# The second batch's norm, transposes and projections four steps sooner in a hand-written order of layer 0's attention

## The chip, the cores and the metric

The kernel runs on one core of a Trainium2 chip. The metric is the device time of one execution in microseconds (us), the median of several runs. Before the change it is 1410.35 us over three runs (1407.18 to 1412.27).

## The reference, cut to what matters

Four blocks of a small network follow each other on an activation of 4 batches x 256 tokens x 512 features; each adds an attention and a feed-forward result to it. Only the attention of block 0 is touched here:

```python
xn = layernorm(x)                                  # x: (4, 256, 512)
q, k, v = heads(xn @ wq.T), heads(xn @ wk.T), heads(xn @ wv.T)   # 32 heads of 16
q, k = rope(q), rope(k)
scores = where(causal, q @ k.T / sqrt(16), -inf)
out = softmax(scores) @ v
x = x + out @ wo.T + ffn(xn)
```

The four batches are independent of each other up to the sum at the end. The feed-forward part unpacks 4-bit weights; the unpacking is done beside the attention.

## The kernel before, in words

`layer0_attention` (from line 151) runs first, `layer0_ffn` (from line 685) after it, then the other blocks. x is held in eight tiles of 128 tokens, two to a batch. The attention of one batch is cut into four blocks of eight heads, so there are N = 16 blocks, n = 0 to 15, and block n belongs to batch n // 4.

**The order is written out by hand.** Inside `manual_schedule` (line 206) the four compute engines execute their instructions in the order in which the Python code issues them; nothing reorders them. The code walks steps h = -24 to 141 (line 548). `span` is 32 steps, the distance of two batches; two blocks are eight steps apart. In each step the instructions are issued in this order:

1. `selected` (POOL, causal zeroing of one tile of exponentials) for the blocks whose turn it is;
2. the table `first`: scores, transposed maxima, products with the values and what follows them;
3. whatever was booked for this step with `at(h, ...)` in the dictionary `due`: this is where norms, transposes and projections stand;
4. the table `then`: `masked` (DVE, mask and row maximum, two instructions of each of four score tiles);
5. `exponentials` (ACT);
6. in odd steps above 0, one item of `aside`: unpacking of the feed-forward weights, first eight pairs of nibble instructions (line 634) at h = 1 to 15, at h = 17 three DVE instructions (lines 639 to 643) with two stores, from h = 19 on a fetch, a nibble (661), a subtraction (670) and so on.

**A block's steps**, counted from 8n: scores of the second half of the queries at -14 (line 380), maxima at -13 to -11; scores of the first half at -10, maxima at -9 and -8; the maxima transposed on PE at -6 (421, `turn_maxima`), `lowered` on ACT at -5 (426), `joined` on POOL at -3 (431); then the transposed scores `st` at 0 and 4 (439, `turned`), exponentials (449) at 0 to 7, the products with the values `av` at 6 and 10 (469), and their transposes and divisions at 7 and 11 (485, 486, 488, `divided`).

**A batch's own work** is booked ahead of its blocks: `turn(h, b)` (line 244) books the norm of its two tiles on DVE at h (140, `normed`), the four pairs of PE transposes at h + 2 and h + 4 (253), and their copies into `xT` at h + 3 and h + 5, alternating between DVE (98) and ACT (96). `features(h, ...)` (275) books one quarter of the q or the k projection: four matmuls at h (282), the rotation on DVE at h + 1 (293, 293, 295, `rotary`), its sum on POOL at h + 2 (302), and for k two scaled copies on ACT at h + 3 (307). `values(h, ...)` (315) books a half of one tile's v projection: four matmuls (322) and at h + 1 one copy on ACT and one on DVE (333, 334). For batches 1 to 3 the call stands at step 2 of the batch before, with the projections from 7 steps later on. `output` (339) books the product with `wo` of the batch before, at step 17 of a batch.

**PSUM.** Scores use six banks with the tag A. Everything else (projections, transposes, transposed maxima, av) goes through `hb()` (220), which hands out the four halves of two tiles, `half_0` and `half_1`, in the fixed order half_1, half_0, half_1, half_0. Waits are set by tile, not by half: an instruction that reads one half of a tile also waits for a write of the other half that stands ahead of it in the written order.

Of the kernel before, what the change touches and what calls it, by code (L numbers as in the profile page):

```python
# [31 lines left out]
B, T, C = 4, 256, 512  # L32
# [23 lines left out]
def block_stack(ctx: ExitStack, tc: tile.TileContext, d: dict, out: bass.AP):  # L56
# [37 lines left out]
    def evac(i, dst, src):  # L94
        if i % 2:
            nc.scalar.copy(dst, src)
        else:
            nc.vector.tensor_copy(dst, src)
# [33 lines left out]
    def normed(t, moments, patterns):  # L132

        xn = lnp.tile([P, C], F32, tag="xn", name=f"xn_{t}")
        dst, src = xn, x_sb[:, t, :]
        if patterns:
            before, after, sizes = patterns
            dst = xn.rearrange(after, **sizes)
            src = src.rearrange(before, **sizes)
        nc.vector.tensor_scalar(dst, src, *moments[t], ALU.subtract, ALU.mult)  # L140
        return xn
# [9 lines left out]
    def layer0_attention(hook, aside, xp, wd):  # L151
# [13 lines left out]
        with (  # L165
# [54 lines left out]
            def hb():  # L220

                turns.append(0)
                return halves[len(turns) * 2 % 4 + len(turns) // 2 % 2]
# [3 lines left out]
            def at(h, *fs):  # L227
                due.setdefault(h, []).extend(fs)
# [15 lines left out]
            def turn(h, b):  # L244

                for k, t in enumerate((2 * b, 2 * b + 1)):
                    had = {}

                    def half(c0, t=t, had=had):
                        tp = had[c0] = hb().rearrange("p (c i) -> p c i", c=2)  # L250
                        for c in range(2):
                            f = slice((c0 + c) * P, (c0 + c + 1) * P)
                            nc.tensor.transpose(tp[:, c, :], had["xn"][:, f], ident)

                    def copy(c0, t=t, had=had):
                        evac(c0 // 2, xT[:, c0 : c0 + 2, t * P : (t + 1) * P], had[c0])

                    at(h, lambda t=t, had=had: had.update(xn=normed(t, mom, patterns)))
                    for c0 in (0, 2):
                        at(h + 2 + 2 * k, lambda c0=c0, f=half: f(c0))  # L260
                        at(h + 3 + 2 * k, lambda c0=c0, f=copy: f(c0))
# [234 lines left out]
            span = 8 * NC  # L496

            def halves_of_x():
                x = [
                    xp.tile([P, NC, 512], F32R, tag=f"x{i}", name=f"x_{n}_{i % 2}")  # L500
                    for i, n in enumerate(("hi", "hi", "lo", "lo"))
                ]
                return x[:2], x[2:]

            def split(half, c):
                x = xT[:, c, half * 512 : half * 512 + 512]
                eng = (nc.vector, nc.gpsimd)[half]
                nc.scalar.copy(hi[half][:, c], x)
                eng.tensor_tensor(lo[half][:, c], x, hi[half][:, c].bitcast(F32), ALU.subtract)

            end = 8 * N + 6
            batches = [Batch(0)]
# [34 lines left out]
            with start_order:  # L547
                for h in range(-24, end + 8):
                    b, k = divmod(h, span)
                    if k == 2 and 0 <= b < B - 1:  # L550


                        turn(h, b + 1)
                        batches.append(Batch(b + 1))
                        u, h0 = batches[-1], h + 7
                        for i in range(4):
                            u.features(h0 + 2 * i, i % 2, i // 2)
                        for i in range(2):
                            u.features(h0 + 16 + 2 * i, i, 2)
                            u.values(h0 + 20 + 2 * i, i, 0)  # L560
                            u.features(h0 + 24 + 2 * i, i, 3)
                            u.values(h0 + 28 + 2 * i, i, 1)
                    if k == (17 if b < 3 else 14) and 1 <= b < B:

                        for i in range(4):
                            batches[b - 1].output(h + (2 if b < 3 else 4) * i, i // 2, i % 2)
                    if h == 8 * N - 22:
                        hi, lo = halves_of_x()
                        for i in range(8):
                            at(h + 2 * i, lambda i=i: split(i % 2, i // 2))  # L570
                    if (h + 14) % 8 == 0 and 0 <= (h + 14) // 8 < N:
                        blocks.append(Block((h + 14) // 8))
                    now = [(h - 8 * n, x) for n, x in enumerate(blocks)]
                    for o, x in now:
                        if 0 <= o - 1 < 8:
                            x.selected(*divmod(o - 1, 4))
                    for o, x in now:
                        if o in first:
                            first[o](x)
                    for f in due.pop(h, ()):  # L580
                        f()
                    for o, x in now:
                        if o in then:
                            then[o](x)
                    for o, x in now:
                        if 0 <= o < 8:
                            x.exponentials(o % 4)
                    if h % 2 == 1 and h > 0 and aside:
                        aside.pop(0)()
                assert not aside and not due  # L590
                return hi, lo, [batches[-1].output(None, i // 2, i % 2) for i in range(4)]
# [1540 lines left out]
    with (  # L2132
        tc.tile_pool(name="gu", bufs=1) as gup,
        tc.tile_pool(name="gur", bufs=2) as raw,
        tc.tile_pool(name="gus", bufs=READY) as ready,
        tc.tile_pool(name="guh", bufs=1) as held,
        tc.tile_pool(name="dram", bufs=1, space=bass.MemoryType.DRAM) as dram,
    ):
        gu = GateUp(gup, raw, ready, held, dram)
        aside = []  # L2140

        def hook():
            gu.load()
            aside.extend(gu.points())
            for blk in range(NBLK):
                aside.extend(gu.pieces(blk))

        def layer1_begun():
            pools = [
                early.enter_context(tc.tile_pool(name=n, bufs=k, side="right"))  # L2150
                for n, k in (("w1", 1), ("l1", 1))
            ]
            begun.append(Layer1(layer1_weights(pools[0]), pools[1]))
            return begun[0]

        with tc.tile_pool(name="wd", bufs=1) as wdp, ExitStack() as x2:
            wd = wdp.tile([P, NBLK, C], F32, name="wd")
            xp = x2.enter_context(tc.tile_pool(name="x2", bufs=1, side="right"))
            begin = layer0_attention(hook, aside, xp, wd)
            layer0_ffn(gu, layer1_begun, x2, wd, *begin)  # L2160
# [131 lines left out]
```

## Time and profile before

| | us |
|---|---|
| median of three runs | 1410.35 |
| the profiled execution's own time | 1409.99 |
| its span, first to last instruction | 1408.3 |
| PE busy in the span | 1360.0 (97%) |
| DVE busy | 897.2 (64%) |
| POOL busy | 750.8 (53%) |
| ACT busy | 521.3 (37%) |
| mean granted TensorE clock | 0.985 |

The span starts with the first instruction; times in the text are counted from there. The attention with its first projections takes the first 272 us or so: the first matmul of the feed-forward part (line 767) starts at 271.75. The first block's `st` (h = 0) starts on PE at 37.89 us. PE executes one projection (four fp32 matmuls) as eight recorded passes, so "x8" in a row is one projection, and "x16" of line 439 is one `turned` of a block. A granted clock of 0.50 in a window means that PE ran at half speed there. In a row of the timeline the bracket gives the idle time of that engine just before and what ended it.

### The profile page before, as it was taken

The page shows a single profiled execution, that of the slowest core. Times are in us where ns is not written, and L with a number is a line of the kernel's source. Part 1 is how long each engine was busy: PE and PEld are TensorE (multiplying, and loading weights), DVE is VectorE, ACT ScalarE, POOL GpSimd, SP SyncE. Part 2 cuts the span into 40 slices and gives each one's busy share as a digit, 9 for nine tenths or more (in the row PEclk, how much of TensorE's full clock was granted, in tenths as well). Part 3 has the DMA queues.
Part 4 walks back from the last instruction along what each step waited for, and adds up shares of the span by engine and source line. Part 5 has one row for each costly group of instructions (what it writes and reads, how often), then busy time and mean ns, then how long its engine had stood idle before and what let it go on. Part 6 is the DMA issues. An engine that isn't in the chain of part 4 may idle for free.

```text
span 1408.3 us, 20885 instructions
## 1 busy us (share of the span) xinstructions
PE 1360.0 (97%) x7332; PEld 1069.7 (76%) x7332; DVE 897.2 (64%) x2361; ACT 521.3 (37%) x1338; POOL 750.8 (53%) x772
## 2 busy tenths in 40 slices
PE   8889999899998999999999999999999999999998
PEld 7556666578545667888888888888888888877887
DVE  7677778478928249635756756565566655768654
ACT  2434335378202212332333432333333344545430
POOL 3445546467646105864777857868558675321210
PEclk9899999899999999999999999999999999999999
DMA  5021222300510021011311203212113000403001
GB/s 196 2 58 35 46 46 66 96 0 1 168 63 16 0 83 47 30 46 35 98 46 64 68 16 94 68 46 64 53 61 105 19 27 1 135 0 113 1 1 61
DMA packets 51033, 76.54 MB, mean 54 GB/s; under 512 B 16506, under 2 KB 23829, under 8 KB 50544
## 3 DMA queue, kind: packets, MB, share of 16 engines
q1 hardware_dynamic: 50000, 74.16, 17.1%
q8 instruction: 58, 0.95, 0.3%
q10 hardware_dynamic: 816, 0.79, 0.2%
q14 instruction: 47, 0.39, 0.1%
q0 software_dynamic: 112, 0.26, 0.1%
HBM read 67.28 MB, written 7.91 MB: 53 GB/s over the span
## 4 chain that ended last, share of the span: by engine, by line
PE 85%; DVE 10%; ACT 2%; issue 2%; POOL 1%; DMA 1%; SPq 0%; DVEq 0%; ACTq 0%; POOLq 0%
PE m L1379 18%; PE m L1343 15%; PE dn L735 5%; PE gu L767 5%; PE s L1735 4%; PE av L1808 4%; PE half L282 4%; PE m L1365 3%; PE m L1355 3%; PE s L1739 2%; PE l1o L1016 2%; PE av L1809 2%; PE st L439 2%; DVE masked L393 2%; PE half L322 2%
## 5 line engine op out<-in xcount | busy, mean ns | idle before, releaser
L1783 POOL TENSOR_TENSOR p<-p,rs 128x512 f32<-128x512 f32 (+1 forms) x128 | 107.0, 857 | 149.5 <-DVE rs L1780 138.2
L1769 ACT ACTIVATE p<-p,nm 128x256 f32<-128x256 f32 (+1 forms) x256 | 113.3, 443 | 107.5 <-DVE nm L1753 107.2
L1437 DVE TENSOR_TENSOR x_sb<-x_sb,m 128x512 f32<-128x512 f32 x82 | 55.9, 685 | 82.4 <-PE m L1379 67.4
L1343 PE MATMUL m<-xT,wq_b 128*128 128x256 f32 x448 | 103.9, 380 | 3.6 <-DVE x_sb L1603 2.2
L1753 DVE CUSTOM_DVE_ANT_0 p<-s,cmask 128x256 f32<-128x256 f32 (+1 forms) x256 | 76.1, 353 | 47.5 <-PE s L1735 45.5
L1403 POOL TENSOR_TENSOR q<-q,t 128x512 f32<-128x512 f32 x64 | 82.2, 1286 | 31.5 <-DVE t L1394 28.2
L393 DVE CUSTOM_DVE_ANT_0 masked<-s,cmask 128x256 f32<-128x256 f32 (+1 forms) x256 | 89.8, 351 | 11.2 <-PE s L380 1.6
L1817 ACT COPY o<-av 128x512 f32<-128x512 f32 x64 | 37.5, 586 | 157.2 <-PE av L1809 157.2
L1326 POOL TENSOR_TENSOR c<-c,z 128x512 f32<-128x512 f32 x28 | 36.4, 1300 | 105.9 <-DVE c L1323 49.3
L1343 PEld LDWEIGHTS m<-xT,wq_b 128*128 128x128 f32 x448 | 82.1, 190 | 14.0 <-DVE x_sb L1603 2.6
L453 POOL TENSOR_SCALAR_AFFINE_SELECT keys<-keys 128x256 f32<-128x256 f32 x128 | 56.7, 454 | 65.1 <-ACT keys L449 63.7
L1379 PE MATMUL m<-wo_b,o 128*128 128x256 f32 x384 | 89.6, 379 | 0.0
L1394 DVE TENSOR_TENSOR t<-m,rope_sb 64x512 f32<-64x512 f32 (+1 forms) x144 | 86.2, 599 | 2.0
L449 ACT ACTIVATE keys<-st 128x384 f32<-128x384 f32 x128 | 57.3, 488 | 77.0 <-PE st L439 77.0
L1801 ACT COPY q<-pT 128x512 f32<-128x512 f32 x64 | 37.5, 585 | 122.6 <-PE pT L1792 120.6
L735 PE MATMUL dn<-wd,hT 128*128 128x512 f32 x176 | 76.4, 593 | 2.3 <-DVE sb L782 2.3
L787 POOL TENSOR_TENSOR sa<-sa,sb 128x1024 f32<-128x1024 f32 x22 | 62.0, 2823 | 30.5 <-DVE sb L782 30.5
L1343 PE MATMUL m<-x_s,wq_t 128*128 128x256 f32 x320 | 77.1, 386 | 1.1 <-ACT kv L1428 1.1
L1379 PEld LDWEIGHTS m<-wo_b,o 128*128 128x128 f32 x384 | 71.3, 190 | 8.8
L1343 PEld LDWEIGHTS m<-x_s,wq_t 128*128 128x128 f32 x320 | 60.8, 193 | 10.5 <-ACT kv L1428 1.5
L1808 PE MATMUL av<-q,kv 128*128 128x512 f32 x128 | 65.5, 593 | 0.6 <-ACT q L1802 0.6
L1735 PE MATMUL s<-kv,q 128*128 128x256 f32 x256 | 65.8, 379 | 0.0
(333 smaller groups left out, 3442.3 us busy)
## 6 DMA issues: line engine op xcount, KB each, us to landing
wq_b<-in_wq SPq DMA_DIRECT2D x38, 256.0 KB, 3.0
wo_b<-in_wo SPq DMA_DIRECT2D x32, 256.0 KB, 2.6
raw<-in_wo SPq DMA_DIRECT2D x16, 512.0 KB, 3.6
wkv_b<-in_wkv SPq DMA_DIRECT2D x16, 256.0 KB, 2.8
wos_d<-wos_row SPq DMA_DIRECT2D x28, 128.0 KB, 2.8
gate_q<-in_gate_q SPq DMA_DIRECT2D x11, 256.0 KB
up_q<-in_up_q SPq DMA_DIRECT2D x11, 256.0 KB
wq3s_b<-in_wq SPq DMA_DIRECT2D x8, 256.0 KB, 3.2
```

The source lines that it names most:

```text
L393: nc.vector.tensor_tensor_reduce(out=ap.tile([P, T], F32, tag="masked", name="masked", bufs=1)[:, 0:n], in0=self.s[part][i][:, e, :], in1= ...
L735: nc.tensor.matmul(po, lhsT=hT[:, k, t * P : (t + 1) * P], rhs=wd[:, k, :], start=k == 0, stop=k == NBLK - 1,)
L767: nc.tensor.matmul(p[:, half], lhsT=w[:, g, :], rhs=x[half][:, g], start=k == 0, stop=k == 1,)
L1343: nc.tensor.matmul(out[:, i, :], lhsT=b[:, c, i * P : (i + 1) * P], rhs=a[:, c, :], start=start and i == 0 and c == 0, stop=i == 1 and c == 1,
L1379: nc.tensor.matmul(out[:, t, :], lhsT=a[:, c, t * P : (t + 1) * P], rhs=b[:, c, :], start=start and t == 0 and c == 0, stop=t == 1 and c = ...
L1394: nc.vector.tensor_tensor(t2[at], src[of], sin[of], ALU.mult)
L1403: after(1 + 2 * pause, lambda: nc.gpsimd.tensor_tensor(dst, dst, t2, ALU.add))
L1735: nc.tensor.matmul(s1[:, i, :], lhsT=q[:, i, P:T], rhs=kt[:, 0, :], start=True, stop=True)
L1753: nc.vector.tensor_tensor_reduce(out=x[f"p{part}"][:, e, :], in0=x[f"s{part}"][:, e, :], in1=cmask if part else cmask[:, P : 2 * P], scale ...
L1769: nc.scalar.activation(p, p, AF.Exp, bias=x["nm"][:, part, e : e + 1], scale=-1.0, accum_out=x["sums"][:, part, e : e + 1],)
L1783: nc.gpsimd.tensor_tensor(p, p, bc(x["rs"][:, part, :], 2, n), ALU.mult)
L1808: nc.tensor.matmul(av, lhsT=v[:, 0:P], rhs=x["q0"], start=True, stop=False)
```

## The change

In the walk over h the booking of a batch's own work is reached at other steps. The second batch is booked at h = -2 instead of h = 2; the third and fourth stay where they are, at h = 34 and h = 66. Nothing else is edited: the number of instructions, their operands and all other bookings are the same.

```diff
                 for h in range(-24, end + 8):
                     b, k = divmod(h, span)
-                    if k == 2 and 0 <= b < B - 1:
-                        turn(h, b + 1)
-                        batches.append(Batch(b + 1))
+                    if h in (-2, span + 2, 2 * span + 2):
+                        turn(h, len(batches))
+                        batches.append(Batch(len(batches)))
                         u, h0 = batches[-1], h + 7
                         for i in range(4):
                             u.features(h0 + 2 * i, i % 2, i // 2)
                         for i in range(2):
                             u.features(h0 + 16 + 2 * i, i, 2)
                             u.values(h0 + 20 + 2 * i, i, 0)
                             u.features(h0 + 24 + 2 * i, i, 3)
                             u.values(h0 + 28 + 2 * i, i, 1)
```

So for the second batch:

| | step before | step after |
|---|---|---|
| norms | 2 | -2 |
| transposes | 4, 6 | 0, 2 |
| copies to xT | 5, 7 | 1, 3 |
| q and k, first two quarters | 9, 11, 13, 15 | 5, 7, 9, 11 |
| q and k, third quarter | 25, 27 | 21, 23 |
| v, first half | 29, 31 | 25, 27 |
| q and k, last quarter | 33, 35 | 29, 31 |
| v, second half | 37, 39 | 33, 35 |

The third batch's norms stay at 34, its transposes at 36 and 38.

## Prediction, made before the changed kernel was run

> **What bounds the kernel now.** I read the page's busy shares first: PE is busy for 97% of the span, so the kernel is a chain of PE work, and a change pays only where PE stands still or runs at half clock. Next the chain that ended last: up to 272 us it changes between PE and DVE rows of the attention, so this stage is on the path. Then the windows, cut where `st` (L439) of steps 0, 8, 16, 24, 32, 40 and 48 starts or nearly ends on PE:
>
> ```profile
> core 0: us, PE busy (x) PEld busy (x) DVE busy (x) ACT busy (x) POOL busy (x), PEclk, DMA share, GB/s
> 37.89:50.05 12.16, 9.43 (x77) 5.61 (x76) 8.63 (x42) 7.11 (x16) 6.29 (x10) 0.86 0.00 1
> 50.05:68.03 17.98, 17.50 (x113) 11.29 (x113) 11.48 (x64) 5.80 (x14) 7.63 (x15) 0.81 0.01 2
> 68.03:79.46 11.43, 8.90 (x87) 5.36 (x87) 10.21 (x43) 5.69 (x14) 6.81 (x13) 1.00 0.32 73
> 79.46:95.64 16.18, 15.52 (x111) 9.95 (x111) 12.11 (x54) 6.07 (x15) 8.93 (x18) 0.89 0.25 50
> 95.64:116.89 21.25, 18.46 (x139) 12.30 (x138) 14.86 (x61) 7.39 (x20) 8.75 (x15) 0.92 0.18 38
> 116.89:130.40 13.51, 12.53 (x99) 8.32 (x99) 10.56 (x47) 5.77 (x14) 7.88 (x14) 1.00 0.13 30
> ```
>
> The reader is to see the unequal loads. Call the rows A to F. A and C hold no projection and PE idles 2.7 and 2.5 us in them; B holds four; E holds four and the third batch's transposes too, and takes 21.25 us. The clock column is below 1 in A, B, D and E: one-microsecond windows put the half clock at 44.75-47.5, 51.3-58.1, 82.5-85.8 and 102.8-106, 16 us in all. Last the timeline of PE, then of DVE:
>
> ```profile
> 42.48 0.70 PE L439 MATMUL st<-q_e,k_e 32*128 32x256 f32 x4 [0.65 <-DVE maxima L393]
> 43.52 0.89 PE L439 MATMUL st<-q_e,k_e 32*128 32x256 f32 x10 [0.34 <-DVE maxima L393]
> ...
> 52.40 3.78 PE L282 MATMUL half<-xT,wq_sb 128*128 128x256 f32 x8
> ...
> 62.75 1.99 PE L282 MATMUL half<-xT,wq_sb 128*128 128x256 f32 x8
> ...
> 71.28 0.44 PE L421 MATMUL half<-ident,maxima 128*128 128x128 f32 x2 [1.41 <-DVE maxima L393]
> ...
> 102.50 3.68 PE L282 MATMUL half<-xT,wk_sb 128*128 128x256 f32 x8 [1.77 <-DVE tr L485]
> ```
>
> ```profile
> 48.75 0.45 DVE L485 STREAM_TRANSPOSE tr<-half 128x256 f32<-128x256 f32 x1 [2.15 <-PE half L253]
> ...
> 58.28 0.42 DVE L293 TENSOR_TENSOR qs<-half,rope_sb 128x256 f32<-128x256 f32 x1 [5.76 <-PE half L421]
> ```
>
> A projection costs 1.92 us at full clock and 3.7 at half (62.75 against 52.40). In A PE waits for DVE's maxima; at 58.28 DVE has stood 5.76 us behind one slow projection. From there to 82.7 DVE stands 0.3 us in all: B's second half and C are DVE's.
>
> **The change part by part.** Moved are 2 norms (DVE, 0.65 us from start to start), 8 transposes (PE, 0.15), 4 copies to xT (0.34), 12 projections (PE, 1.92), 8 rotations (DVE, 1.01 for three instructions), 8 sums (POOL, 0.73), 4 pairs of scaled copies (ACT, 0.91), 4 ACT and 4 DVE copies of v (0.27, 0.21). No count changes and no DMA is issued by them. SP's queue keeps its order; the unpacking and its fetches keep their steps. On POOL only the sums pass some `keys` selections (0.4 each), and POOL is busy 6.3 of 12.2 us in A. On ACT the copies and scaled copies pass exponentials: 7.1 of 12.2. I cost both at nothing beyond what follows; uncovered, a sum would cost 0.73 and a pair 0.91 where a score waits for it.
>
> *A, steps 0 to 8.* The norms fill a DVE wait (0.88 us before 36.56); the maxima end 0.3 later. L421 of step 2 writes the tile that the copy of step 1 reads, and starts at about 40.55 instead of 39.94. The copy of step 3 now stands on DVE in front of the maxima of block 2 and waits until PE has done four scores (1.07) and two transposes: behind it the maxima start at 42.8 instead of 41.43. On ACT, `lowered` waits for the same tile: last exponential of the first half at 44.3 instead of 41.9. `st` of step 4 waits for both and ends at 45.75 instead of 44.34. This is the new wait, 1.4 us. Then come projection q (1.92), av 0.79, scores 0.64, projection k 1.92 (its rotation's read is over by then), so `st` of step 8 could start at 51.0, against 50.05.
>
> The clock: the Trainium skill, "TensorE: Matmul & The Clock Gate", section "HAM oscillation — how this bites in real kernels", says to leave no PE gap over about 3.4 us. No gap here is over 1.8, so by the rule A would run at full clock and end at 51.0. The rows show half clock after gaps of 0.84, 0.65 and 0.34. I go by the row, let 2.8 us of half clock fall on q as they fell at 44.75 before, and lose 1.4: **A ends at 52.4, 2.3 late, with two projections done.**
>
> *B, steps 8 to 16*, loses two projections (3.84 PE) and two rotations (2.0 DVE). From 45.75 on PE has no gap, and I expect no second half clock: q ends at 55.3, av and L421 at 56.5, and the rotation that now stands here starts at 56.55, where the first one started at 58.28. DVE from there to L421 of step 18 took 13.0 us (58.28 to 71.28); less two rotations, of which about 0.4 goes to waits, it is 10.6-11.0: **67.2 instead of 71.28, 4.1 ahead.** By the skill's rule (51.0) it would be 5.5; with the second half clock kept (6.8 us, costing 3.4) 0.7.
>
> *C, steps 17 to 24*, gains q, k (3.84 PE) and one rotation ahead of its end. PE has 2.5 us of gaps; DVE has none. Laid behind 75.71: q to 77.6, av and scores to 79.2, k after q's rotation 79.0-80.9, `st` to 82.0 instead of 81.06. **Cost 1.0, bounds 0.5 and 3.84.** The fetch chain at 72-77.24 (stores, loads, then the 0.3 wait of L661) is covered by the same 4.9 us of maxima as before.
>
> *D* has four projections before and after, v v q k for q k v v. With C's gaps filled the half clock at 82.5-85.8 should go: gain 1.6, bounds 0 and 1.6. The wait of 0.54 for `tr` in front of the second projection becomes about 0.1, as a copy (0.21) stands there for a rotation: 0.4. I take **1.6 + 0.4**, less than that if the clock stays.
>
> *E, steps 32 to 40*, loses two projections (3.84) and two rotations (2.0); v, v stay with the third batch's norms and transposes. The `tr` wait falls from 1.77 to about 1.0. DVE work from 99.7 on: copy 0.2, norms 1.3, tr 0.6, maxima 1.9, nibble 0.5, copy 0.2, maxima and gather 2.2, copy 0.3, subtraction 1.0, tr 0.6, copy 0.3, maxima 2.7, nibble 0.5, in sum 12.3, plus 1 of waits: 13.3 instead of 18.05 (99.69 to 117.74). **Gain 4.8.** But PE then has only 9 us of work in 13, as sparse as C was, and a half clock is likely behind it, on the third batch's first q, as C's was on q at 82.5: 1.6 back. So 3.2, bounds 2.5 and 4.8.
>
> From step 41 on nothing is moved; F and all later rows keep their lengths.
>
> Sum: 4.1 - 1.0 + 2.0 + 3.2 = 8.3. Of D's clock term I believe half (0.8): **7.5 us.** The bounds together, 0.7 - 3.84 + 0 + 0.4 + 2.5 = -0.2 (slower) to 5.5 - 0.5 + 2.0 + 4.8 = 11.8. The profiled execution took 1409.99 (span 1408.3 and 1.7 around it), so 1402.5; the median of before is 0.36 above it: **1402.8 us.**
>
> **The rivals.** *Absorbed:* the second half clock stays (lead 0.7 at step 18), C pays 3.84, D keeps its clock (0.4), E gains 4.8: 2.1, so 1408.2. For it: C is DVE's, and DVE has no room. Against: PE's 2.5 us of gaps in C. *Nothing:* the attention ends by its last blocks or by fetches, 1410.3. Against: PE's rows follow each other from 131 to 235 with gaps under 1.8 and DMA share is about 0.2. *Slower, by the clock:* the lighter start keeps PE's clock at half. One microsecond of it costs 0.5. If it held from 45.75 to 68, some 22 us instead of the 2.8 assumed, 9.7 is lost, and two half clocks more in E (6.8 us, 3.4) make it 13.1: 7.5 - 13.1, or 1416. It decides from 15 us of additional half clock on. For it: 16 us of half clock stand in the trace after gaps this small. Against: from q at step 5 on PE has more to do than before.
>
> **How the numbers follow.** Forecast (gain 4.2 to 11.8) 0.69; absorbed 0.16; nothing 0.05; slower 0.10, of which nine tenths beyond 0.3%. About 0.3%, 4.2 us, is what a measurement of this kernel can tell from no change. So faster 0.69, within 0.22, slower 0.09. The range, 1398.5 (the upper bound of the gain) to 1409.5 (absorbed, and somewhat over half of the way from there to nothing), leaves out the slower case and most of nothing.
>
> **What would show it.** After: the first q projection at 45.8-46 and L421 of step 18 near 67; no DVE wait of over 2 us before step 16; clock 1.00 in most of 50 to 60; `st` of step 24 ending near 78, of step 40 near 108; E 16-18 us long; the start of L767 near 264. It is wrong if maxima wait behind the copies of steps 1 and 3 for over 2 us, if C grows by its full 3.84, or if E's gain returns as half clock in F.

## The result and the profile after

The changed kernel takes 1399.93 us, the median of 12 runs, beside 1408.21 us of 12 runs of the kernel before. The ratio on record is 0.9959, with a 95% interval of 0.9941 to 0.9976: 5.8 us faster (3.4 to 8.3), against 7.5 forecast. (The two medians lie 8.3 us apart, the two means 6.3; the text goes by the ratio.)

The profiled execution of after is one of its longer ones: eight of the 12 runs lie at 1397.6 to 1401.0 with a mean granted clock of 0.988 to 0.992, four at 1406.5 to 1409.0 with 0.982 to 0.984, and the profiled one took 1406.50 (span 1404.8, clock 0.984). Against the profiled execution of before (1409.99, clock 0.985) it is 3.5 us faster. They have nearly the same amount of half clock (42.8 and 44.8 us), though not in the same places, so they can be compared stage by stage.

From here on the stages are cut where `st` (L439) of steps 8, 16, 24, 32, 40 and 48 *ends* on PE, in every kernel alike. The windows of after, stages C to F in this cut (us of the stretch, its length, then the busy time of each engine with its instructions, granted clock, DMA share, GB/s):

```profile
67.61:83.78 16.17, 15.95 (x99) 9.62 (x99) 9.41 (x38) 4.58 (x12) 6.94 (x13) 0.62 0.19 51
83.78:97.07 13.29, 13.29 (x115) 9.05 (x115) 11.37 (x51) 6.12 (x16) 7.42 (x14) 1.00 0.26 62
97.07:113.03 15.96, 13.34 (x108) 8.92 (x107) 13.34 (x58) 7.21 (x19) 7.88 (x13) 0.93 0.22 50
113.03:129.92 16.89, 15.91 (x115) 10.51 (x115) 11.03 (x45) 5.58 (x15) 8.27 (x15) 0.87 0.09 24
```

D and E, which were 15.46 and 20.38 us, are 13.29 and 15.96. But C, which was to be the cheap place for two more projections, is 16.17 instead of 12.10: its clock column stands at 0.62, where before had 1.00. Here are the ends of `st` in the profiled executions, in us from the span's start, and the stage that each closes:

| end of `st` of step | 8 (A) | 16 (B) | 24 (C) | 32 (D) | 40 (E) | 48 (F) | start of the feed-forward |
|---|---|---|---|---|---|---|---|
| before | 52.47 | 69.02 | 81.12 | 96.58 | 116.96 | 131.67 | 271.75 |
| after | 53.44 | 67.61 | 83.78 | 97.07 | 113.03 | 129.92 | 269.88 |
| after is ahead by | -0.97 | 1.41 | -2.66 | -0.49 | 3.93 | 1.75 | 1.87 |

The lead comes to nothing twice, in C and half of it in F, and the 1.87 us that are left at the start of the feed-forward stay to the end. The rest of the 3.5 is no effect of the order: before has 3.4 us at half clock at 1310 us, long after the attention, which after has not.

The timeline of PE in after, around the two places where the forecast set its numbers:

```profile
43.84 1.82 PE L439 MATMUL st<-q_e,k_e 32*128 32x256 f32 x14 [0.64 <-DVE maxima L393]
45.59 3.56 PE L282 MATMUL half<-xT,wq_sb 128*128 128x256 f32 x8
...
62.19 0.70 PE L380 MATMUL s<-kT,qT 32*128 32x256 f32 x4 [0.31 <-DVE maxima L393]
63.24 0.77 PE L380 MATMUL s<-kT,qT 32*128 32x256 f32 x4 [0.35 <-DVE maxima L393]
64.96 2.65 PE L439 MATMUL st<-q_e,k_e 32*128 32x256 f32 x16 [0.94 <-DVE maxima L393]
...
68.98 0.69 PE L421 MATMUL half<-ident,maxima 128*128 128x128 f32 x2
...
102.50 1.99 PE L322 MATMUL half<-wv_sb,xT 128*128 128x256 f32 x8 [1.27 <-DVE tr L485]
```

and of DVE:

```profile
42.46 0.42 DVE L98 COPY xT<-half 128x256 f32<-128x256 f32 x1 [1.81 <-PE half L253]
...
56.55 0.43 DVE L293 TENSOR_TENSOR qs<-half,rope_sb 128x256 f32<-128x256 f32 x1 [1.29 <-PE half L421]
```

The 1.81 us at 42.46 are the new wait of stage A. The first slow projection (45.59, 3.56 us) and the rotation at 56.55 stand where the forecast put them. Then, between 61.9 and 65, PE waits three times for maxima; these gaps are not in the forecast, and some 1.4 us after the last of them (64.96 to 66.3) the clock falls. One-microsecond windows of after show where it falls and where it returns:

```profile
66.00:67.00 1.00, 1.00 (x12) 0.95 (x12) 0.79 (x7) 0.00 (x0) 0.88 (x3) 0.67 0.00 0
...
79.00:80.00 1.00, 1.00 (x13) 0.49 (x16) 0.83 (x4) 0.00 (x0) 0.24 (x1) 0.51 0.00 0
80.00:81.00 1.00, 1.00 (x21) 0.47 (x13) 0.74 (x2) 0.00 (x0) 0.00 (x0) 1.00 0.00 0
```

That is 13.6 us at half clock, from 66.3 to 80, almost all of C.

Idle time alone does not decide it. Here are the 3.41 us of after that end at this fall, and the 3.41 us around the longest gap of PE (1.27 us, ending at 102.50):

```profile
62.92:66.33 3.41, 2.09 (x12) 1.24 (x16) 3.13 (x20) 1.74 (x5) 3.32 (x6) 1.00 0.01 2
100.46:103.87 3.41, 2.13 (x14) 1.24 (x7) 3.17 (x10) 2.29 (x6) 1.36 (x3) 1.00 0.46 112
```

PE is busy for as long in both, and behind the second the clock stays at 1.00. The work differs: the first stretch holds only scores and `st`, whose rows say 32*128 (32 rows of operands), the second also a projection (128*128). The same holds in all 14 profiles. Between 38 and 280 us the clock falls 58 times. In the 3.41 us before a fall PE is busy for 37 to 89% of the time, but with matmuls on 128 rows for at most 29%. Of 836 other stretches of this length, after which the full clock stayed, only 29 have so little. No run was made to test this, so it is an observation and not a proven cause.

### The profile page after: what moved, and what is told of

Read it like the earlier page. It is cut to its first block, busy times and chain, and to the rows that moved or that the text cites. A ratio compares the mean times of both kernels' runs of the same rounds, so it can differ in the third digit from the quotient of the medians.

```text
span 1404.8 us, 20880 instructions
## 1 busy us (share of the span) xinstructions
PE 1359.4 (97%) x7332; PEld 1069.6 (76%) x7332; DVE 897.9 (64%) x2361; ACT 520.7 (37%) x1338; POOL 749.3 (53%) x772
## 4 chain that ended last, share of the span: by engine, by line
PE 85%; DVE 9%; ACT 2%; issue 1%; POOL 1%; DMA 1%; SPq 0%; DVEq 0%; ACTq 0%; POOLq 0%
PE m L1380 18%; PE m L1344 15%; PE dn L736 5%; PE gu L768 5%; PE s L1736 4%; PE av L1809 4%; PE half L282 3%; PE m L1366 3%; PE m L1356 3%; PE st L439 2%; PE s L1740 2%; PE av L1810 2%; PE l1o L1017 2%; PE half L322 2%; PE half L347 1%
## 5 line engine op out<-in xcount | busy, mean ns | idle before, releaser
L1754 DVE CUSTOM_DVE_ANT_0 p<-s,cmask 128x256 f32<-128x256 f32 (+1 forms) x256 | 76.1, 353 | 47.5 <-PE s L1736 45.5
L736 PEld LDWEIGHTS dn<-wd,hT 128*128 128x128 f32 x176 | 33.1, 190 | 42.9 <-issue 39.7
```

Source lines behind the costliest of these rows:

```text
L736: nc.tensor.matmul(po, lhsT=hT[:, k, t * P : (t + 1) * P], rhs=wd[:, k, :], start=k == 0, stop=k == NBLK - 1,)
L1754: nc.vector.tensor_tensor_reduce(out=x[f"p{part}"][:, e, :], in0=x[f"s{part}"][:, e, :], in1=cmask if part else cmask[:, P : 2 * P], scale ...
```

## The experiments

**Theory:** the forecast's. A lead won in A and B and the relief of D and E both reach the end, C costs about 1 us. **Rival 1:** only the relief of E counts; the lead of A and B is lost in C. **Rival 2:** the order matters little, and the time follows the amount of half clock. The ratio is to before on the same chip; before was 1406.83 us in the first group of runs (e1 to e4), 1407.65 in the second (e5 to e8) and 1407.03 in the third (e9 to e12). Stage lengths in the profiled executions, for reference:

| | A+B, to step 16 | C | D | E | F | ratio [95% interval] |
|---|---|---|---|---|---|---|
| before | 69.02 | 12.10 | 15.46 | 20.38 | 14.71 | 1 |
| after | 67.61 | 16.17 | 13.29 | 15.96 | 16.89 | 0.9959 [0.9941, 0.9976] |
| e1, first four projections sooner | 67.02 | 13.60 | 15.26 | 18.70 | 14.90 | 0.9998 [0.9986, 1.0011] |
| e2, the other eight sooner | 69.84 | 14.27 | 13.28 | 15.24 | 14.70 | 0.9936 [0.9913, 0.9959] |
| e6, the last four sooner | 67.91 | 12.25 | 20.65 | 15.22 | 16.40 | 0.9993 [0.9972, 1.0015] |
| e7, the third quarter sooner | 70.23 | 15.66 | 14.11 | 18.70 | 14.71 | 1.0000 [0.9979, 1.0021] |
| e8, e2 with later turns sooner | 69.36 | 19.82 | 13.30 | 12.77 | 16.35 | 0.9993 [0.9980, 1.0005] |
| e10, after with fillers | 64.88 | 12.66 | 13.29 | 15.96 | 17.05 | 0.9930 [0.9908, 0.9952] |

### Each half of the change alone (e1, e2)

e1 books norms, transposes and the first four projections of the second batch sooner, the other eight where before has them:

```diff
+                        h1 = h0 + (4 if h < 0 else 0)
-                            u.features(h0 + 16 + 2 * i, i, 2)
+                            u.features(h1 + 16 + 2 * i, i, 2)
...
```

(and the same in the three calls after it.)

> Norms, transposes, copies and the first four projections of the second batch four steps sooner, the other eight where they stood (steps 25 to 39). Theory (idle PE time is filled at the start, and the steps 32 to 40 are relieved): only the first part is there, L421 of step 18 near 67-69, E as long as before (20-21 us); 3 to 4 us faster than before, about 1404.5. Rival (only the length of the half clock differs between the kernels, the places of the projections bring nothing): the time follows the mean granted clock on the line of the kernel before, whatever was moved.

Measured: 1406.97 us, ratio 0.9998 [0.9986, 1.0011]. The theory's 3 to 4 us are not there. The windows of e1 in C and E:

```profile
67.02:80.62 13.60, 13.38 (x83) 7.50 (x83) 8.98 (x40) 4.89 (x13) 6.86 (x12) 0.50 0.30 62
...
95.88:114.58 18.70, 16.07 (x123) 10.67 (x123) 14.02 (x58) 7.10 (x19) 8.33 (x14) 1.00 0.19 43
```

e1 reaches step 16 at 67.02, 2.0 ahead. Then all of C runs at 0.50: its half clock lasts from 66.3 to 83.4, 17.1 us. C holds no projection here, as in before, and takes 1.5 longer all the same; at step 32 the lead is 0.7. E is not as long as before's 20.38, as was expected, but 18.70: before has 3.4 us of half clock in it, this execution none. So this one execution is 2.2 ahead at step 48; the 22 runs together show no such lead.

e2 does the opposite: norms, transposes and the first four projections where before has them, the other eight as in after.

```diff
-                        turn(h, len(batches))
+                        turn(h + (4 if h < 0 else 0), len(batches))
-                        u, h0 = batches[-1], h + 7
+                        u, h1 = batches[-1], h + 7
+                        h0 = h1 + (4 if h < 0 else 0)
...
-                            u.features(h0 + 16 + 2 * i, i, 2)
+                            u.features(h1 + 16 + 2 * i, i, 2)
...
```

> Only the other eight projections four steps sooner (21 to 35); norms, transposes and the first four as before (2 to 15). Theory: A and B as before, C about 1 us longer, D 0 to 2 shorter, E about 4 shorter with up to 1.6 of half clock given back in F: 3 to 4 us faster than before, about 1404.5. Rival: as before at an equal clock, 1408.

Measured: 1399.10 us, ratio 0.9936 [0.9913, 0.9959], 9.0 us faster: all of the gain of after, and perhaps more. The windows of e2, C and E:

```profile
69.84:84.11 14.27, 12.49 (x100) 8.34 (x99) 11.81 (x52) 5.68 (x14) 7.64 (x15) 0.88 0.28 59
97.39:112.63 15.24, 12.62 (x107) 8.16 (x107) 12.64 (x56) 7.00 (x19) 7.89 (x13) 1.00 0.22 49
```

C and D together take 27.55, to the hundredth near the 27.56 of before, and E 5.1 less. Between e1 and e2 rival 1 fits, and the theory's first term falls. How much of E's 5.1 is the order's can be read where E has no half clock: it takes 18.70 with all its projections (e1, e7, e9) and 15.22 to 15.24 with two fewer (e2, e6, e11), so 3.5 is the order's. The other part of e2's gain goes with less half clock (last table).

### Norms and transposes alone, and half the distance (e3, e4)

e3 keeps only norms, transposes and copies sooner; all 12 projections stand where before has them:

```diff
-                        u, h0 = batches[-1], h + 7
+                        u, h0 = batches[-1], h + (11 if h < 0 else 7)
```

> Only norms, transposes and copies four steps sooner, all twelve projections as before. Theory: the new wait of A alone (maxima of block 2 behind the copy of step 3, 1.4 us), against 1.2 us of transposes that no longer stand at steps 4 and 6: no difference beyond 1 us, 1408 to 1409. Rival: as before at an equal clock, 1408.

Measured: 1404.24 us, ratio 0.9985 [0.9965, 1.0005]: a small gain or none, and no loss worth the name. e4 books the second batch at h = 0, two steps sooner than before instead of four:

```diff
-                    if h in (-2, span + 2, 2 * span + 2):
+                    if h in (0, span + 2, 2 * span + 2):
```

> The whole booking at step 0, two steps sooner instead of four. Theory: A gets one projection, C one, E keeps three: about half of the gain, 3 to 4 us, 1404.5. Rival: as before at an equal clock, 1408.

Measured: 1407.60 us, ratio 0.9997 [0.9982, 1.0012]. There is no half gain at half the distance. Its profile has 53.2 us of half clock, before's 42.8, and its 14 runs have 43.6 on average against 40.5; what else keeps it from gaining was not taken apart.

### Which of the eight (e6, e7)

e6 is e2 with only `features(..., 3)` and `values(..., 1)` sooner (last quarter of q and k, second half of v); e7 is e2 with only `features(..., 2)` sooner (third quarter).

```diff
-                            u.features(h0 + 24 + 2 * i, i, 3)
-                            u.values(h0 + 28 + 2 * i, i, 1)
+                            u.features(h1 + 24 + 2 * i, i, 3)
+                            u.values(h1 + 28 + 2 * i, i, 1)
```

> Only the last four projections of the second batch four steps sooner (29, 31, 33, 35 instead of 33 to 39); the other eight, norms and transposes as before. So E loses two projections and D gains two; C stays empty. Theory (the gain needs both ends: E relieved and C's idle PE time used): D is PE's, so it grows by 3.8, E shrinks by 4 to 5: 0 to 1.5 us faster than before. Rival (E's relief alone is the gain): 5 us or more faster, like the run with all eight.

> Only the third quarter's q and k four steps sooner (21, 23 instead of 25, 27); C gains two projections, D loses two, E stays as before. Theory: C costs 1 to 2, D shrinks by 3.8 or less, half clock at 82 to 86 goes: 2 to 4 us faster than before. Rival (E's relief alone is the gain): no difference beyond 1 us.

e6: 1406.18 us, ratio 0.9993 [0.9972, 1.0015]; e7: 1409.21 us, 1.0000 [0.9979, 1.0021], a miss. The windows of e6 in D and E:

```profile
80.16:100.81 20.65, 19.33 (x131) 13.39 (x131) 11.83 (x52) 5.91 (x16) 8.27 (x15) 0.87 0.18 39
100.81:116.03 15.22, 12.61 (x107) 8.14 (x107) 12.63 (x53) 6.99 (x19) 7.88 (x13) 1.00 0.23 51
```

E is as short as in e2 (15.22), but D now holds six projections and is 5.2 longer (5.2 us of D are at half clock, against 3.4 in before): the load is only handed on. The windows of e7 in C and D:

```profile
70.23:85.89 15.66, 14.13 (x102) 8.93 (x106) 12.87 (x53) 5.68 (x14) 7.69 (x14) 0.78 0.22 54
85.89:100.00 14.11, 12.36 (x99) 7.68 (x99) 9.72 (x48) 6.23 (x16) 7.03 (x13) 0.88 0.26 56
```

With the third quarter alone C is filled (+3.6), with 6.8 us of half clock in it where before has none. D is relieved to two projections and hardly shortens (-1.4): PE waits 0.98 us for maxima there, at 87.65, and 3.4 us are at half clock. E's load is what it was. Of the orders tried only those gain clearly that do both at once: two projections out of E, and two into C, with D passing through four.

### Relieving E further (e8)

In e2, E still holds the third batch's norms and transposes. e8 books these (and the fourth batch's) 16 steps sooner:

```diff
+                    if h in (2, span - 14, 2 * span - 14):
+                        turn(h, (2, span - 14, 2 * span - 14).index(h) + 1)
...
-                        turn(h + (4 if h < 0 else 0), len(batches))
```

> The run with the other eight projections four steps sooner, and besides it norms, transposes and copies of the third and fourth batch 16 steps sooner (booked at 18 and 50 instead of 34 and 66), so that they no longer stand among four projections at steps 32 to 40 and 64 to 72. Theory: E and the same stretch 32 steps later shrink by 2 to 4 us each, C grows by up to 2: 3 to 5 us faster than the run with the other eight alone, about 1395. Rival (only the half clock counts): as that run at an equal clock, 1399.

Measured: 1406.99 us, ratio 0.9993 [0.9980, 1.0005]: a miss, and all of e2's gain is lost. The window of e8 in C:

```profile
69.36:89.18 19.82, 16.41 (x108) 10.33 (x107) 13.06 (x54) 6.45 (x17) 8.19 (x14) 0.83 0.19 43
```

E does shrink, to 12.77 (2.5 less than in e2), but C takes in the same work at a price of 5.6 (19.82 against 14.27). Its half clock lasts 6.8 us there instead of 3.4, and DVE, busy for 13.06 us, stands still in front of one of the copies that were moved in:

```profile
81.75 0.42 DVE L98 COPY xT<-half 128x256 f32<-128x256 f32 x1 [4.62 <-PE half L282]
```

It waits for a projection written to the same tile, which ran at half clock. In this order C has room for two projections, not for norms, copies and transposes as well.

### Holding the clock (e5, e9, e10, e11)

If A and B's lead is lost only because the clock falls in C, then PE work in the gaps, useless but cheap, should keep the clock and let the lead through. e5 is after with four matmuls of the identity at steps 15, 17 and 19, between `due` and `then`:

```diff
+                    if h in (15, 17, 19):
+                        for _ in range(4):
+                            nc.tensor.matmul(hb()[:, 0:P], lhsT=ident, rhs=ident, start=True, stop=True)
```

> The changed kernel with twelve 128-column matmuls of the identity more, four each at steps 15, 17 and 19, whose results nobody reads; nothing is left out. They stand where PE waits for DVE's maxima in C. Theory, as it stands after the first four runs (the lead of A and B is real but is paid back in C, where PE now idles longer and falls to half clock): less half clock between 66 and 80 us in the profile, mean half clock per run 5 to 10 us shorter than in the changed kernel (33.6), and 1.5 to 3 us less time, though 3.6 us of PE work are added. Rival (half clock falls by chance): half clock as in the changed kernel and a time 0 to 3 us longer.

> The kernel before with the same twelve matmuls of the identity at steps 15, 17 and 19; nothing else. If the filler helps only where the lightened B and C fall to half clock (theory), the kernel before, whose C has no half clock in its profile (only 82 to 86 behind it), gains at most that piece, 0 to 2 us. Rival (the filler would help any of these kernels as much, so the changed kernel with filler says nothing of the change): 4 us or more, half clock per run 10 us below that of before.

e5: 1398.87 us, ratio 0.9936 [0.9912, 0.9959]. Its timeline of PE:

```profile
65.53 1.16 PE L585 MATMUL half<-ident 128*128 128x128 f32 x8
66.62 2.00 PE L439 MATMUL st<-q_e,k_e 32*128 32x256 f32 x16
...
74.86 1.99 PE L282 MATMUL half<-xT,wq_sb 128*128 128x256 f32 x8
```

The `st` behind the first filler takes 2.00 us instead of 2.65, and the projection at 74.86 1.99 instead of 3.78 (the one at 75.34 in after): the half clock of 66 to 80 is gone. C takes 12.67, with 3 x 1.16 = 3.5 us of useless work in and around it. The runs have 22.4 us of half clock on average, after's 33.6. Against after the time is 1.1 us less by the medians and 3.3 by the means, where 1.5 to 3 were expected; the intervals of the two ratios overlap. The same lines in before (e9) give 1407.40 us, ratio 1.0004 [0.9984, 1.0023]: they bring nothing where C ran at 1.00 anyway. (In e9 and in e11 the filler of step 15 overwrites one quarter of k of the second batch ahead of its rotation, so these two give other results; the order and amount of the rest are the same.)

e10 has the fillers at steps 105, 107, 109 and 111 as well, where after and before both have 13.7 us of half clock near 240 to 255; e11 puts the same seven fillers into e2.

```diff
+                    if h in (15, 17, 19, 105, 107, 109, 111):
```

> The changed kernel with the filler at steps 15, 17, 19 and at 105, 107, 109, 111 besides, in front of the half clock that every profile so far but two shows for 13.7 us from about 240 on. Theory: that stretch shortens to 3 to 7 us, 2 to 4 us less than with the first filler alone, about 1396. Rival: the stretch stays, 1400.

> The run with the other eight projections four steps sooner (first four, norms and transposes as before), with both fillers. It has E's relief without A's and B's part. Theory: with the clock held, the lead of A and B survives in the changed kernel, so this one is 1.5 to 3 us slower than the changed kernel with both fillers. Rival (A and B bring nothing even then): the same time within 1 us.

e10: 1397.58 us, ratio 0.9930 [0.9908, 0.9952]; e11: 1398.09, 0.9936 [0.9912, 0.9960]. The window of e10 in C:

```profile
64.88:77.54 12.66, 12.28 (x115) 8.38 (x115) 10.25 (x41) 4.90 (x13) 7.22 (x13) 1.00 0.32 67
```

C is at 1.00 and 12.66 long. e10 leads e11 by 3.6 us at steps 16 to 32 (64.88 against 68.45; 90.83 against 94.41). That is not the order alone: in A and B e11 has 6.8 us of half clock and e10 none. e5, whose order up to step 16 is that of e10, has 6.8 us there too and reaches step 16 at 68.62, no sooner than e11. In F e10 falls to 0.86 (6.8 us of half clock at 104 to 112) and e11 does not: at step 48 the lead is 0.5 (123.84 against 124.34), and in the median of the runs it is 0.5 as well, less than the intervals can tell from nothing and less than the 1.5 to 3 expected. Against e5 the later fillers bring 1.3 us by the medians, where 2 to 4 were expected.

e10 is the best version by its median. It beats before; by its mean it is 4.2 us below after (1397.7 against 1401.9, standard error 1.3), though the two were timed on different occasions and the intervals of their ratios overlap.

### The new wait of stage A (e12)

The DVE wait of 1.81 us at 42.46 was the one loss that the forecast saw in A. e12 is e10 with the second batch's copies to xT one step later, at 2 and 4:

```diff
-                        at(h + 3 + 2 * k, lambda c0=c0, f=copy: f(c0))
+                        at(h + 3 + 2 * k + (h < 0), lambda c0=c0, f=copy: f(c0))
```

> The changed kernel with both fillers, and the second batch's copies to xT one step later (2 and 4 instead of 1 and 3), so that the copy of the second tile no longer stands on DVE in front of block 2's first maxima. Theory (that copy is the new wait of A): DVE's wait of 1.8 before 42.5 goes, st of step 4 ends about 1 us sooner, 0.5 to 1.5 us faster than with both fillers alone. Rival (the wait costs nothing, something else is as late): the same within 0.5 us.

Measured: 1399.46 us, ratio 0.9940 [0.9917, 0.9962]: no faster. The timeline of DVE in e12:

```profile
41.46 0.42 DVE L98 COPY xT<-half 128x256 f32<-128x256 f32 x1 [0.32 <-PE half L421]
42.51 0.42 DVE L393 CUSTOM_DVE_ANT_0 masked<-s,cmask 128x256 f32<-128x256 f32 x1 [0.63 <-PE s L380]
```

and the end of `st` of step 4 on PE:

```profile
45.91 1.09 PE L439 MATMUL st<-q_e,k_e 32*128 32x256 f32 x10 [0.64 <-DVE maxima L393]
```

The wait of 1.81 is now 0.32 and 0.63, yet `st` of step 4 ends no sooner (6.4 us after that of step 0, in e10 6.2): its last instructions still wait 0.64 us for maxima.

### Half clock and time over all runs

Each run has a span and a mean clock c, from which the microseconds at half clock follow as 2 x (1 - c) x span. Over the 265 runs of these 14 kernels, the span grows by 0.33 us for each microsecond of half clock *within one kernel* (correlation 0.96). With that slope the kernels can be set to the same 35 us:

| | runs | mean span | mean half clock | span at 35 us |
|---|---|---|---|---|
| before | 107 | 1405.6 | 40.5 | 1403.8 |
| e1 | 22 | 1405.1 | 42.2 | 1402.8 |
| after | 12 | 1400.2 | 33.6 | 1400.6 |
| e2 | 6 | 1397.5 | 26.6 | 1400.3 |
| e3 | 14 | 1403.9 | 37.5 | 1403.1 |
| e4 | 14 | 1405.9 | 43.6 | 1403.1 |
| e5 | 8 | 1396.9 | 22.4 | 1401.1 |
| e6 | 14 | 1405.3 | 38.4 | 1404.2 |
| e7 | 14 | 1406.1 | 38.8 | 1404.9 |
| e8 | 22 | 1405.4 | 38.6 | 1404.2 |
| e9 | 14 | 1405.9 | 35.8 | 1405.7 |
| e10 | 6 | 1395.9 | 17.2 | 1401.8 |
| e11 | 6 | 1396.7 | 20.0 | 1401.7 |
| e12 | 6 | 1397.3 | 20.5 | 1402.1 |

(The 107 runs of before are those of the three groups; the 12 of after were timed on another occasion. The scatter around the slope makes the standard error of the last column 0.25 for after, 0.35 for e2 and 0.2 for e1.) Of the 5.4 us between the means of before and after, 3.2 are there at equal half clock, and 2.3 are 6.9 us less half clock at 0.33. So rival 2 is right for a little under half; for e2 it is over half, 4.6 of 8.1. At equal half clock e2 gains 3.5, as E does at full clock, and e6 and e7 nothing, as in the medians. But e1, e3 and e4 are 0.7 to 1.0 ahead, which would fit a small lead of A and B; more half clock hides it in the times of e1 and e4. With fillers the order's part shrinks (they cost PE time) and the clock's part grows. That the clock makes the time and does not merely go with it rests on e5 and e10, which add PE work and nothing else and have shorter stages.

## Why the prediction was right, and where it was wrong

**Direction and size hold**: 5.8 us against 7.5, and 1399.93 us lies in the range of 1398.5 to 1409.5. The sum behind it holds in part.

- *A.* The steps after are within 0.3 us: L421 of step 2 at 40.31 (40.55), maxima of block 2 at 42.80 (42.8), `st` of step 4 to 45.66 (45.75), a slow first projection, `st` of step 8 from 52.50 (52.4). Here the trace was the better guide than the rule of the Trainium skill on gaps over 3.4 us, which would have let A end at 51.0. e12 shows that the copy's wait, called the cause of the 1.4 us, was not alone: without it another wait ends `st`. One reading of before was short: the half clock at 44.75 to 47.5 lasts from 44.5 to 47.9, so 3.4 us and not 2.8, and the four pieces come to 17.1 us and not 16.
- *B.* The rotation stands at 56.55 to the hundredth. L421 of step 18 starts at 68.98, not 67.2, so it is 2.3 ahead, not 4.1.
- **The step that failed** is "From 45.75 on PE has no gap, and I expect no second half clock". From 50 to 66 the clock is 1.00 indeed, but PE, with two projections less in B, catches up with the maxima: gaps of 0.31, 0.35 and 0.94 us at 62 to 65, and a half clock from 66.3 to 80. The forecast followed DVE through the second part of B and never asked what PE does there with two projections less; for E it asked just that. The rule on gaps over 3.4 us does not cover this either, as no gap here is near it. A later section of the Trainium skill, "TensorE: Matmul & The Clock Gate", "A second HAM failure mode: psum-queue depth-cycling", tells of a kernel whose frequent short idle times between groups of matmuls sent the clock back and forth. That is nearer to the rows here, but the two stretches shown above have equal idle time, and only one is followed by half clock.
- *C* cost 4.1 us, over its upper bound of 3.84. At full clock the term was right: with the fillers the stage is 12.66 or 12.67, 0.6 over before. What was taken from DVE's room was right, what the clock takes was missing.
- So of A and B's 4.1 nothing reaches the end in the runs as timed (e1: 0.9998), and 1.0 us at equal half clock. This is the part of the rival "absorbed" that came true, by another way: not C's room was short, but its clock.
- *D* gained 2.2 (2.0 forecast), as the half clock at 82.5 went. *E* gained 4.4 (4.8), with the wait for `tr` at 1.27 (1.0); of such a gain 3.5 is the order's and the rest before's own half clock in E. *F* gave 2.2 back as half clock (1.6 forecast). These hold. In the profiled execution E less F is 2.2, against 3.2.
- "Nothing moved from step 41 on" holds for the order, not for the clock. The feed-forward starts at 269.88 (264 forecast), and about 2.3 of the 5.4 us between the means go with less half clock, some of it far behind the attention, which no step of the sum had.

By the profiled execution alone, the order gives 1.75 us of the 7.5 up to step 48. The medians differ by more, since the other executions of after have less half clock; at equal half clock it is 3.2. So the direction was foreseen for the right reason (E), and the size is near in part by luck: the lead that did not come is partly replaced by less half clock elsewhere.

**Open** stays why one kernel's executions differ so much in half clock (after: 1397.6 to 1409.0 us), why e2's and after's runs have less of it than before's, and whether the small gain of e3 and e4 at equal half clock is real.

## What to carry to other kernels

In an order written by hand, look for the stretch where two loads meet and move one of them into a stretch where the in-order engines stand; check that both ends move, or the load is only handed on (e6, e7). A lead that is won ahead of a sparse stretch is worth what the clock lets through: look at what PE does in the stretch that was lightened, how long and on how many rows, and not only in the one that was filled. When a change is worth 0.5%, compare many runs by their granted clock as well as by time.

## What the hardware showed that was not expected

- Half clock came in multiples of 3.4 us in all profiles: 3.4, 6.8, 10.2, 13.6, 17.1 (but for the piece that the end of the span cuts off). The Trainium skill, "TensorE: Matmul & The Clock Gate", section "🔬 Part 1: The HAM clock gate (the "warmup" mystery)", states a window of 3413 ns, and the lengths agree. But the longest gap of PE between 38 and 132 us is 1.27 us in after and 1.77 in before: half clock came without any long gap, behind stretches with few matmuls on 128 rows.
- A microsecond of half clock cost 0.33 us of time, not the 0.5 that PE work alone would give. That part of it lies beside waits for DVE is likely, but no run separates it.
- Useless PE work made the kernel no slower and probably faster: with 3.5 us of identity matmuls (e5) the 13.6 us of half clock in C are not in the profile, nor are they in those of e10 and e12.
- The half clock near 240 to 255, in both kernels, is gone in the three profiles with the later fillers (e10, e11, e12). Of the other eleven, seven have 13.7 us there, three 6.8 to 10.2, and e6 has none, so it can also stay away without fillers. The windows of after and of e10 there:

```profile
240.00:255.00 15.00, 14.53 (x66) 9.42 (x69) 6.78 (x29) 5.91 (x14) 6.79 (x11) 0.54 0.40 113
```

```profile
230.00:260.00 30.00, 26.56 (x254) 17.44 (x247) 20.40 (x65) 14.07 (x34) 22.11 (x35) 1.00 0.48 130
```

After has 0.54 there, e10 1.00 over a wider stretch.
